# A two-layer cross-attention block on one core: scores of two heads in neighbouring PSUM banks, one exponential for both, and normalised tokens written by GpSimd

## The chip, the core and the metric

The kernel runs on one core of a Trainium2 chip. The metric is device time in microseconds for one launch. Five engines work side by side, each through its own queue in order: TensorE (PE, with its weight loads PEld) multiplies matrices into PSUM, VectorE (DVE) and ScalarE (ACT) read PSUM and SBUF, GpSimd (POOL) works on SBUF, and SyncE (SP) issues DMAs. PSUM has eight banks of 512 float32 columns in each of 128 partitions; each matmul here writes within one bank.

## What is computed

Two layers, each a transformer block with self-attention, cross-attention to a context, and a gated feed-forward part, for 4 batches of 512 tokens of 320 features. There are 20 heads of 16 features. The context has 1601 rows of 192 features.

```python
h1 = _ln(x, n1_g, n1_b)
x = _attn(h1, h1, q1, k1, v1, o1_w, o1_b, heads) + x
h2 = _ln(x, n2_g, n2_b)
x = _attn(h2, context, q2, k2, v2, o2_w, o2_b, heads) + x
h3 = _ln(x, n3_g, n3_b)
a, g = jnp.split(h3 @ ff_w1 + ff_b1, 2, axis=-1)
x = a * jax.nn.gelu(g, approximate=False) @ ff_w2 + ff_b2 + x
```

`_attn` projects q, k and v, takes `softmax(q k^T / 4)` for each head over all keys (512 in self-attention, 1601 in cross-attention), multiplies by v and projects the result. Everything is float32.

## The kernel before

**Units.** The work of a layer is cut into units (L329, L355 to L361): 20 self units and 20 cross units, one for each batch and group of four heads, and then four feed-forward units, one for each batch. `main` (L1196) runs an attention unit, `ff_main` (L1307) a feed-forward unit. An attention unit goes through its keys in chunks of 128: 4 chunks in self-attention, 13 in cross-attention. All 512 queries of the batch are the columns.

**A chunk** has two rounds (L1264), the first for heads 0 and 1, the second for heads 2 and 3. The four heads of a group sit in four slots of 32 partitions, so that matmuls of four heads can run in TensorE at once. A float32 value is split into a high and a low part that lie in neighbouring rows, and a product takes two passes. For a head, `score` (L1202) takes a PSUM bank, writes keys x queries into it in two passes (L1209), subtracts each query's maximum in a third (L1212), and ACT takes the exponential from that bank into a place in SBUF (L1222, 128x512). In the same round two heads of a later unit get a block of the scores from which their maxima are found: two passes on TensorE (L1021) into a bank each, and a reduction on DVE out of it (L1040, 128x512 to 128x1). So the maxima of a unit are ready before the unit begins. The passes of the round's four heads are interleaved by hand (`round_of`, L1186). After the two rounds of a chunk, `values` (L1229) multiplies the exponentials of the chunk *before* with v for all four heads into one bank (L1236); a column of ones beside v gives the sums. ACT copies that bank to a place (L1252, for the first chunk straight into `o`, L1247), and GpSimd adds the place to the unit's `o` (L1253). In the unit ahead of a feed-forward stage (`last`) there are no maxima, all four heads' scores are in one round, and DVE does the adding (L1249).

**What runs beside.** Layer norm, the projections of q, k and v, the transposed context, the division by the sums and the output projection wait in chains of small steps, each with a cost and a due time. `steps` (L460) runs at the end of each chunk and takes steps by due time as long as a credit lasts; a *light* step is a small piece of DVE work, and `steps` is told how many light ones it may take in the chunk (L1276). The order on all engines is therefore written by the program itself; nothing reorders it later.

**Layer norm** (`add_norm`, L521) takes statistics on DVE (L530), a root by Newton steps that run mostly on GpSimd (L503), writes normalised tokens `hn` on DVE (L546, four instructions of 128x320 a batch and stage, with four of 128x64 more ahead of a feed-forward unit), transposes them on TensorE (L559), and ACT puts scale and offset on them out of PSUM (L566). New parts of q and k are copied out by ACT (L818, L848, L892), split into high and low on GpSimd (L699, L700) and moved by DMAs to their slots.

**Banks.** `bank` (L159) takes the bank of the eight that `Pace` (L54) believes free first. `Pace` keeps a running estimate of the time at which each engine reaches each instruction. The choice changes only which bank is taken, not the order of the instructions.

**Places in SBUF.** One ring of places (L230 to L241) serves the exponentials and ACT's copies: 7 of its own with 2 borrowed ones in self-attention, or 5 borrowed ones in cross-attention, where the weights of self-attention are no longer needed. `o` has three buffers.

Of the kernel before, what the change touches and what calls it, by code (L numbers as in the profile page):

```python
# [9 lines left out]
F32 = mybir.dt.float32  # L10
# [43 lines left out]
class Pace:  # L54


    def __init__(self):
# [3 lines left out]
        self.bank_of = {}  # L61
# [4 lines left out]
    def first(self):  # L66
        i = min(range(8), key=lambda i: self.free[i])
        assert self.free[i] < 1e8, self.bank_of
        return i

    def give(self, i, t):
        self.bank_of = {n: k for n, k in self.bank_of.items() if k != i}
        self.bank_of[t.tensor.name] = i
        self.opens[i] = self.free[i]
        self.free[i] = 1e9

    def unread(self, t):
        b = self.bank_of[t.tensor.name]
        self.free[b] = self.ready[b]

    def see(self, r):
        i = r.ins
        kind = type(i).__name__
        banks = {self.bank_of.get(x.bass_ap.tensor.name) for x in list(i.ins) + list(i.outs) if hasattr(x, "bass_ap")}
        banks.discard(None)
# [41 lines left out]
def kernel(ctx: ExitStack, tc: tile.TileContext, x, context, ws, out):  # L127
# [67 lines left out]
    def load_x(b):  # L195
# [40 lines left out]
    at_place = {"kind": "self", "i": -1}  # L236

    def place():
        these = places[at_place["kind"]]
        at_place["i"] = (at_place["i"] + 1) % len(these)  # L240
        return these[at_place["i"]]  # L241
# [160 lines left out]
    def step_bank(shape, name):  # L402
        return bank(name, shape)

    def warm(n):

        ps = step_bank([P, 512], "wps")
        for _ in range(n):
            see(nc.tensor.matmul(ps[:, : 4 * P], lhsT=ident, rhs=fill, start=True, stop=True))
        pace_of.unread(ps)  # L410
# [110 lines left out]
    def add_norm(l, b, i, put, done, due):  # L521
# [19 lines left out]
        def normalise(t):  # L541
# [3 lines left out]
            for to, at, n in ((0, 0, D), (D, D - REST, REST))[: 1 + i // 2]:  # L545
                see(nc.vector.tensor_scalar(  # L546
                    s["hn"][:, t, to : to + n], xb[:, t, at : at + n],
                    s["mv"][:, t, 0:1], s["rstd"][:, t : t + 1], ALU.subtract, ALU.mult,
                ))
            s["round"] = clock["round"]  # L550

        def turn(k, at, n):
# [3 lines left out]
            ps = step_bank([P, N], "hps")  # L556
# [67 lines left out]
    def add_context(l, b, put, due, free):  # L624
# [39 lines left out]
        def tail():  # L664
            ps = step_bank([P, 2, P], "cps")
# [87 lines left out]
    def add_proj(u):  # L753
# [47 lines left out]
        def queries(part):  # L801
            w = N // 2 // parts
            at = [i * (N // 2) + part * w for i in range(2)]
            ps = step_bank([P, 512], "qps")
# [29 lines left out]
        def keys():  # L834

            ps = step_bank([P, 512], "kps")
# [38 lines left out]
        def keys_of_context(i):  # L875

            pss = [bank("kps") for _ in range(4)]
# [705 lines left out]
```

## Time and profile before

| | |
|---|---|
| median of 3 runs | 3033.34 us (3026.81 to 3038.23) |
| the profiled execution's own time | 3038.45 us |
| its span, first to last instruction | 3036.6 us |
| mean granted TensorE clock | 0.989 |
| busy: PE, DVE, ACT, POOL | 2945.4, 2049.5, 1957.7, 1326.4 us |

The stages, by the lines and tiles that are in use: self-attention of the first layer until about 411 us, cross-attention until about 1240, feed-forward until about 1540, then the second layer with self-attention until about 1900, cross-attention until about 2740 and feed-forward to the end.

How to read the rows quoted below: a row of a grouped view has the line, the engine, the operation, what it writes and reads, the shape and the count; then busy us, the mean ns of one, the idle time of the engine just before, and what ended it. A row of the timeline has the start in us, the length, and the instructions merged into it. In TensorE's rows a float32 matmul of the values product counts as two, and a matmul's end is modelled, so that one which is held up looks longer.

### The profile page before, as it was taken

The page shows a single profiled execution, that of the slowest core. Times are in us where ns is not written, and L with a number is a line of the kernel's source. Part 1 is how long each engine was busy: PE and PEld are TensorE (multiplying, and loading weights), DVE is VectorE, ACT ScalarE, POOL GpSimd, SP SyncE. Part 2 cuts the span into 40 slices and gives each one's busy share as a digit, 9 for nine tenths or more (in the row PEclk, how much of TensorE's full clock was granted, in tenths as well). Part 3 has the DMA queues.
Part 4 walks back from the last instruction along what each step waited for, and adds up shares of the span by engine and source line. Part 5 has one row for each costly group of instructions (what it writes and reads, how often), then busy time and mean ns, then how long its engine had stood idle before and what let it go on. Part 6 is the DMA issues. An engine that isn't in the chain of part 4 may idle for free.

```text
span 3036.6 us, 93325 instructions
## 1 busy us (share of the span) xinstructions
PE 2945.4 (97%) x37842; PEld 1609.5 (53%) x37842; DVE 2049.5 (67%) x4011; ACT 1957.7 (64%) x4029; POOL 1326.4 (44%) x1499
## 2 busy tenths in 40 slices
PE   8989999999999999999998999999999999999999
PEld 4445555555555555455554555555555555544555
DVE  6677788888878888422256778778778878873221
ACT  3666667888887888611136775778878878884101
POOL 3456444554555454301124563545645654542100
PEclk8999999999999999999999999999999999999999
DMA  4434222221222221300113332212211221212000
GB/s 101 106 78 95 62 57 47 66 46 45 60 51 57 44 52 25 93 11 0 32 44 76 85 81 59 53 48 42 52 47 35 52 59 33 49 22 73 14 11 13
DMA packets 223751, 157.80 MB, mean 52 GB/s; under 512 B 152724, under 2 KB 187928, under 8 KB 223320
## 3 DMA queue, kind: packets, MB, share of 16 engines
q1 hardware_dynamic: 222440, 150.78, 21.2%
q8 instruction: 297, 4.87, 0.7%
q10 hardware_dynamic: 880, 1.06, 0.2%
q14 instruction: 134, 1.10, 0.1%
HBM read 44.18 MB, written 9.24 MB: 18 GB/s over the span
## 4 chain that ended last, share of the span: by engine, by line
PE 60%; DVE 8%; issue 1%; ACT 1%; SPq 1%; DMA 1%; POOL 0%; ACTq 0%; POOLq 0%; DVEq 0%
PE av L1236 14%; PE fps L1331 9%; PE st L1209 8%; PE sps L1021 7%; PE yps L1386 6%; DVE pm L1040 5%; PE kps L883 3%; PE fps L1344 2%; PE ops L1153 2%; PE st L1212 2%; PE vps L975 2%; PE qps L807 2%; DVE nmax L1040 2%; PE vps L957 1%; PE kps L840 1%
## 5 line engine op out<-in xcount | busy, mean ns | idle before, releaser
L1040 DVE TENSOR_REDUCE pm<-sps 128x1 f32<-128x512 f32 x1920 | 1191.4, 681 | 108.5 <-PE sps L1021 101.4
L1021 PE MATMUL sps<-kT,q 32*128 32x512 f32 (+1 forms) x6400 | 1063.1, 403 | 24.0 <-DMA kT<-stage 6.3
L1222 ACT ACTIVATE pr<-st 128x512 f32<-128x512 f32 (+1 forms) x1710 | 906.4, 603 | 215.1 <-PE st L1212 210.4
L1209 PE MATMUL st<-q,kT 32*128 32x512 f32 (+1 forms) x5440 | 933.0, 435 | 5.3 <-ACT stage L848 2.6
L1253 POOL TENSOR_TENSOR o<-o,pr 128x512 f32<-128x512 f32 x359 | 461.0, 1284 | 656.3 <-ACT pr L1252 638.6
L1209 PEld LDWEIGHTS st<-q,kT 32*128 32x128 f32 (+1 forms) x5440 | 479.0, 180 | 358.1 <-ACT pr L1222 141.7
L1236 PE MATMUL av<-pr,vals 128*32 128x512 f32 (+1 forms) x3420 | 641.5, 614 | 26.4 <-DVE pm L1040 8.8
L1021 PEld LDWEIGHTS sps<-kT,q 32*128 32x128 f32 x6400 | 548.5, 184 | 129.5 <-DVE pm L1040 24.7
L1212 PE MATMUL st<-m,units 32*128 32x512 f32 (+1 forms) x2720 | 533.1, 392 | 11.9 <-DMA m<-turned 11.9
L1222 ACT ACTIVATE wself<-st 128x512 f32<-128x512 f32 (+1 forms) x867 | 463.3, 604 | 80.0 <-PE st L1212 76.3
L1040 DVE TENSOR_REDUCE nmax<-sps 128x1 f32<-128x512 f32 x640 | 397.3, 681 | 163.0 <-PE sps L1021 152.9
L1236 PE MATMUL av<-wself,vals 128*32 128x512 f32 (+1 forms) x1734 | 369.7, 605 | 11.3 <-DVE pm L1040 5.4
L1253 POOL TENSOR_TENSOR o<-o,wself 128x512 f32<-128x512 f32 x191 | 245.2, 1284 | 301.0 <-ACT wself L1252 289.4
L1331 PE MATMUL fps<-hT,w 128*128 128x512 f32 x640 | 283.3, 596 | 0.0
L1354 ACT ACTIVATE pr<-fps,b 128x512 f32<-128x512 f32 x80 | 54.8, 688 | 341.7 <-PE fps L1344 239.4
L1212 PEld LDWEIGHTS st<-m,units 32*128 32x128 f32 (+1 forms) x2720 | 250.8, 181 | 32.5 <-issue 12.0
L1252 ACT COPY pr<-av 128x512 f32<-128x512 f32 x359 | 218.7, 609 | 24.3 <-PE av L1236 24.0
L1331 PEld LDWEIGHTS fps<-hT,w 128*128 128x128 f32 x640 | 118.9, 190 | 148.3 <-issue 147.5
L1236 PEld LDWEIGHTS av<-pr,vals 128*32 128x32 f32 (+1 forms) x3420 | 91.5, 108 | 195.1 <-DVE pm L1040 108.8
L699 POOL TENSOR_SCALAR stage<-stage 128x256 fp32r<-128x256 f32 (+1 forms) x155 | 106.7, 688 | 147.0 <-ACT stage L818 63.2
L883 PEld LDWEIGHTS kps<-ctxT,w 32*128 32x128 f32 (+1 forms) x4992 | 115.7, 163 | 54.5 <-ACT pr L1222 30.2
L1153 PEld LDWEIGHTS ops<-wo,aT 112*32 112x32 f32 (+1 forms) x3072 | 99.0, 110 | 64.2 <-issue 40.2
(99 smaller groups left out, 3076.9 us busy)
## 6 DMA issues: line engine op xcount, KB each, us to landing
q<-stage SPq DMA_DIRECT2D x314, 128.0 KB
kT<-w SPq DMA_DIRECT2D x240, 104.0 KB
aT<-o SPq DMA_DIRECT2D x320, 32.0 KB
kT<-stage SPq DMA_DIRECT2D x156, 64.0 KB
oturn<-over SPq DMA_DIRECT2D x32, 224.0 KB
kT<-w SPq DMA_DIRECT2D x80, 72.0 KB
w<-in_L_xattn_ff_w_dram SPq DMA_DIRECT2D x20, 256.0 KB
m<-turned SPq DMA_DIRECT2D x318, 4.0 KB
```

The costliest lines, as they stand in the source:

```text
L883: see(nc.tensor.matmul(ps[to : to + n, :PIECE], lhsT=wk_q[rows, k, u.g * GD : u.g * GD + n], rhs=first.kvT[rows, k, at : at + PIECE], star ...
L1021: see(nc.tensor.matmul(out, lhsT=u.q[rows, t // 2, e, t % 2 * P : (t % 2 + 1) * P].bitcast(F32R), rhs=u.kT[rows, keys].bitcast(F32R), star ...
L1040: see(nc.vector.tensor_reduce(to[:, j : j + 1], ps, AX.X, ALU.max, negate=(ns == 1)))
L1153: see(nc.tensor.matmul(ps[f : f + m, : D // 2], lhsT=aT[:n, k, t * P + f : t * P + f + m], rhs=wo[:n, k, cols], start=(k == 0), stop=(k == 2),
L1209: see(nc.tensor.matmul(st[:r, :], lhsT=keys, rhs=u.q[rows, :, e].bitcast(F32R), start=(e == 0), stop=False))
L1212: see(nc.tensor.matmul(st[:r, :], lhsT=units_of[rows, :r].bitcast(F32R), rhs=u.mrow[rows, :].bitcast(F32R), start=False, stop=True,))
L1222: see(nc.scalar.activation(p[:r], st[:r], AF.Exp))
L1236: see(nc.tensor.matmul(ps[j * SLOT : (j + 1) * SLOT, :], lhsT=columns_of[:r, head : head + SLOT], rhs=pr.pop((c, j))[:r, :], start=True, s ...
L1252: see(nc.scalar.copy(vo, ps))
L1253: nc.gpsimd.tensor_tensor(u.o, u.o, vo, ALU.add)
L1331: see(nc.tensor.matmul(ps, lhsT=w1[:, k, i * FF + c * P : i * FF + (c + 1) * P], rhs=u.hT[:, k, :], start=ahead and k == 0, stop=not ahead ...
L1386: see(nc.tensor.matmul(ps[:, :D], lhsT=hid[c][:, t * P : (t + 1) * P], rhs=w2[:, c, :], start=(c == 0), stop=(c == NHC - 1),))
```

## The change

Four things are changed together.

1. All of PSUM is one tile of eight banks. `two_banks` takes a pair of neighbouring banks (0-1, 2-3, 4-5 or 6-7): of the four pairs that one whose later bank `Pace` believes free first. `score` handles two heads at once: their scores lie in a pair of banks, the passes keep their order, and one exponential of 128x1024 reads both banks and writes a pair of places. Single banks are taken as before. The feed-forward unit takes its four banks as two pairs.
2. Places are pairs for the exponentials (4 pairs of its own, one more borrowed in cross-attention) and single ones for ACT's copies (2 borrowed in self-attention, 3 in cross-attention), in two rings of their own. The kernel's own places grow from 7 to 8; `o` has two buffers instead of three.
3. `hn` is written by GpSimd, except at the start of the program.
4. `steps` may take two light steps in each chunk; before it was one in a chunk with extra maxima and in a unit's last chunk.

```diff
-    def bank(name, shape=(P, 512)):
+    wide = ps.tile([P, 8, 512], F32, name="ps")
+    pace_of.name = wide.tensor.name
+
+    def taken():
         i = pace_of.first()
-        t = ps.tile(list(shape), F32, tag=f"bank{i}", name=name)
-        pace_of.give(i, t)
-        return t
+        pace_of.give(i)
+        return i
+
+    def bank():
+        return wide[:, taken()]
+
+    def two_banks():
+        i = min(range(0, 8, 2), key=lambda i: max(pace_of.free[i : i + 2]))
+        assert max(pace_of.free[i : i + 2]) < 1e8, pace_of.free
+        for k in (i, i + 1):
+            pace_of.give(k)
+        return [wide[:, i], wide[:, i + 1]], wide[:, i : i + 2]
...
-    own = const.tile([P, 7, N], F32, name="pr")
-    mine = [own[:, i, :] for i in range(7)]
+    own = const.tile([P, 8, N], F32, name="pr")
+    mine = [own[:, i, :] for i in range(8)]
+    spare = wself[:, : 5 * N].rearrange("p (i n) -> p i n", n=N)
+    ours = [own[:, i : i + 2, :] for i in range(0, 8, 2)]
     places = {
-        "self": mine + [w1_flat[:, (2 * KB + 2) * D : (2 * KB + 2) * D + N], w1r[:, 4 * CTX : 4 * CTX + N]],
-        "cross": mine + [wself[:, i * N : (i + 1) * N] for i in range(5)],
+        ("self", "pairs"): ours,
+        ("self", "single"): [w1_flat[:, (2 * KB + 2) * D : (2 * KB + 2) * D + N], w1r[:, 4 * CTX : 4 * CTX + N]],
+        ("cross", "pairs"): ours + [spare[:, 0:2, :]],
+        ("cross", "single"): [spare[:, i, :] for i in range(2, 5)],
     }
...
-                see(nc.vector.tensor_scalar(
+                eng = nc.vector if start["on"] else nc.gpsimd
+                eng.tensor_scalar(
                     s["hn"][:, t, to : to + n], xb[:, t, at : at + n],
                     s["mv"][:, t, 0:1], s["rstd"][:, t : t + 1], ALU.subtract, ALU.mult,
-                ))
+                )
...
-        def score(c, j):
+        def score(c, heads):
             r = min(P, u.nkeys - c * P)
-            rows = slice(j * SLOT, (j + 1) * SLOT)
-            st = bank("st")
+            sts, both = two_banks()
+            rows = [slice(j * SLOT, (j + 1) * SLOT) for j in heads]
...
             def exponential():
-                p = place()
-                see(nc.scalar.activation(p[:r], st[:r], AF.Exp))
-                pr[c, j] = p
+                p = place("pairs")
+                see(nc.scalar.activation(p[:r], both[:r], AF.Exp))
+                for i, j in enumerate(heads):
+                    pr[c, j] = p[:, i, :]
...
-                u.o = three.tile([P, N], F32, tag="o", name="o")
+                u.o = two.tile([P, N], F32, tag="o", name="o")
...
-                vo = place()
+                vo = place("single")
...
-            steps(None, 1 if extra or c == u.nch - 1 else 2)
+            steps(None, 2)
...
-            return [[bank("fps"), bank("fps")] for e in range(2)]
+            return [two_banks()[0] for e in range(2)]
```

More of the change, by code (lines that the diff above doesn't have):

```diff
@@ L400 @@
     start = {"on": True}
-    def step_bank(shape, name):
-        return bank(name, shape)
     def warm(n):
-        ps = step_bank([P, 512], "wps")
+        i = taken()
         for _ in range(n):
-            see(nc.tensor.matmul(ps[:, : 4 * P], lhsT=ident, rhs=fill, start=True, stop=True))
-        pace_of.unread(ps)
+            see(nc.tensor.matmul(wide[:, i, : 4 * P], lhsT=ident, rhs=fill, start=True, stop=True))
+        pace_of.unread(i)
     def yes():
@@ L875, in keys_of_context @@
         def keys_of_context(i):
-            pss = [bank("kps") for _ in range(4)]
+            pss = [bank() for _ in range(4)]
             for k in range(KB):
@@ L970, in values_of_context @@
             w = (h1 - h0) * DH
-            pss = [bank("vps") for _ in range(4)]
+            pss = [bank() for _ in range(4)]
             for k in range(KB):
@@ L1031, in full_two @@
         def full_two(heads, t, s):
-            pss = [bank("sps") for _ in heads]
+            pss = [bank() for _ in heads]
             if ns == 1:
@@ L1047, in rest_two @@
             w = rest + rest % 2
-            pss = [bank("sps") for _ in heads]
+            pss = [bank() for _ in heads]
             todo = [
@@ L1259, in main @@
             if last:
-                round_of([lambda j=j: score(c, j) for j in range(HG)], [])
+                round_of([lambda heads=heads: score(c, heads) for heads in ((0, 1), (2, 3))], [])
                 tick()
@@ L1268, in main @@
                     extra += rounds
-                    round_of([lambda j=j: score(c, j) for j in ((2, 3) if odd else (0, 1))], pair)
+                    round_of([lambda: score(c, (2, 3) if odd else (0, 1))], pair)
             u.scored = c + 1
```

73 lines of the change are left out of this document (40 added, 33 removed).

## The prediction

> **What bounds the kernel now.** I read the page first (busy shares, chain of waits), then the busy times by stage, then one stretch of the cross stage in order of time.
>
> ```profile
> span 3036.6 us, 93325 instructions
> PE 2945.4 (97%) x37842; PEld 1609.5 (53%) x37842; DVE 2049.5 (67%) x4011; ACT 1957.7 (64%) x4029; POOL 1326.4 (44%) x1499
> PE 60%; DVE 8%; issue 1%; ACT 1%; SPq 1%; DMA 1%; POOL 0%; ACTq 0%; POOLq 0%; DVEq 0%
> ```
> ```profile
> 0.00:411.00 411.00, 377.89 (x5400) 202.59 (x5404) 296.10 (x602) 248.24 (x516) 193.15 (x241) 0.94 0.36 84
> 411.00:1240.00 829.00, 810.84 (x12346) 455.80 (x12346) 671.76 (x1310) 678.18 (x1419) 441.70 (x446) 1.00 0.22 50
> 1560.00:1900.00 340.00, 320.64 (x4792) 172.13 (x4788) 250.84 (x485) 230.02 (x476) 170.84 (x204) 0.97 0.33 75
> 1900.00:2740.00 840.00, 823.08 (x12542) 462.50 (x12535) 668.75 (x1280) 684.02 (x1428) 448.05 (x451) 1.00 0.20 46
> ```
>
> The columns of the second fence are PE, PEld, DVE, ACT, POOL. TensorE holds the chain and is busy 97%. The change leaves its matmuls as they are, in number and size, so all it can win is time in which TensorE waits. In the four attention stages (self, cross, self, cross) TensorE is idle for 33.1 + 18.2 + 19.4 + 16.9 = 88 us. Matmuls that are held up look longer, so some waiting hides inside "busy"; the next rows show how much. DVE and ACT are each busy 81 to 82% of the cross stages, so they are close behind.
>
> ```profile
> 673.55 4.99 DVE L1040 TENSOR_REDUCE pm<-sps 128x1 f32<-128x512 f32 x8 [0.29 <-PE sps L1021]
> 673.83 2.07 ACT L1222 ACTIVATE pr<-st 128x512 f32<-128x512 f32 x4 [0.64 <-PE st L1212]
> 674.30 0.62 PE L1236 MATMUL av<-wself,vals 128*32 128x512 f32 x2
> ...
> 675.30 0.44 PE L1209 MATMUL st<-q,kT 32*65 32x512 f32 x2
> ...
> 675.75 0.62 ACT L1252 COPY wself<-av 128x512 f32<-128x512 f32 x1
> ...
> 676.43 0.49 PE L1021 MATMUL sps<-kT,q 32*128 32x512 f32 x1
> 676.45 1.28 POOL L1253 TENSOR_TENSOR o<-o,wself 128x512 f32<-128x512 f32 x1 [1.06 <-ACT wself L1252]
> ...
> 677.08 1.06 PE L1236 MATMUL av<-pr,vals 128*32 128x512 f32 x8
> ...
> 679.60 1.07 PE L1236 MATMUL av<-wself,vals 65*32 65x512 f32 x8
> ...
> 682.39 1.06 PE L1236 MATMUL av<-pr,vals 128*32 128x512 f32 x8
> ```
> ```profile
> 676.42 0.18 PEld L1021 LDWEIGHTS sps<-kT,q 32*128 32x128 f32 x1 [0.15 <-ACT wself L1252]
> ```
>
> These are three plain chunks (four score heads, four maxima, one values product, nothing else). From one values product to the next they take 677.08 - 674.30 = 2.78, then 2.52, then 2.79 us. The 2.78 has a visible cause: one maximum's matmul at 676.43 needs the bank that the values product used, and ACT's copy out of it ends at 675.75 + 0.62 = 676.37. That copy stood behind four exponentials that began at 673.83. DVE's eight reductions take 4.99, 0.62 each, so four are 2.48 us of a 2.52 us chunk: DVE has no room there either.
>
> **The change part by part.**
>
> *One exponential for 1024 columns.* There are 40 self units of 4 chunks and 40 cross units of 13, 680 chunks with two pairs each: 1360 wide exponentials for 2720. No row shows 1024 columns; rows of other widths bound them.
>
> ```profile
> L1222 ACT ACTIVATE pr<-st 128x512 f32<-128x512 f32 x1616 | 857.0, 604 | 209.9 <-PE st L1212 206.7 <-PE sps L1021 0.8 <-ACT pr L1252 0.3
> L818 ACT ACTIVATE stage<-qps 128x128 f32<-128x128 f32 x80 | 24.2, 302 | 4.4 <-PE qps L807 4.2
> L818 ACT ACTIVATE stage<-qps 128x256 f32<-128x256 f32 x40 | 15.4, 384 | 43.9 <-PE qps L807 36.8 <-DMA q<-stage 2.1 <-DVE stage L700 2.0
> ```
>
> From 128 to 256 columns a column costs (384 - 302)/128 = 0.64 ns, from 256 to 512 (604 - 384)/256 = 0.86 ns. So 512 more columns cost 0.33 to 0.44 us. Today the second exponential of a pair costs (2.07 - 0.60)/3 = 0.49 us. A pair saves 0.05 to 0.16 us; I take 0.06, by the nearer row, that of 256 to 512. That frees 1360 x 0.06 = 82 us of ACT, which is not on the path by itself. What counts is the copy, which comes two pairs, 0.12 us, sooner. How often TensorE waits for this copy:
>
> ```profile
>   ACT pr L1252: 8.0, 50
>   ACT wself L1252: 6.0, 38
> ```
>
> These are two rows of the waits of L1021 (us, times): 88 waits. 88 x 0.12 = **-10.6 us**. Bounds: 0, where DVE is late next, and 88 x 0.27 (2.79 less 2.52) = -24. The 26 chunks just before the feed-forward stages have four exponentials in a row and no maxima: 0 to -3, I take -1.5.
>
> [...]
>
> *Banks in pairs.* The exponential gives both banks back together: the first one 0.33 to 0.44 us later than now, the second a little sooner. The next chunk's scores (675.30) start 1.47 us after the first exponential (673.83). The wide one takes 0.60 + 0.44 = 1.04 at most, so 0.43 us is left and nothing waits. In plain chunks banks fall into two halves: two pairs for scores, and four banks for five takers (four maxima, one values product). The second maximum of a chunk then needs the third reduction, due at 673.55 + 3 x 0.62 = 675.41 while the scores start at 675.30: 0.1 us late for one row group, whose next pass has room. Between 0 and 680 x 0.1 = +68; nearest to the rows above, where such lateness is absorbed: **+3**.
>
> *GpSimd writes the normalised tokens.* 128 instructions, of which the four at the start stay on DVE.
>
> ```profile
> L546 DVE TENSOR_SCALAR hn<-x,mv,root 128x320 f32<-128x320 f32 x96 | 53.9, 582 | 21.0 <-POOL root L510 21.0
> L699 POOL TENSOR_SCALAR w<-w 128x416 fp32r<-128x416 f32 x80 | 100.1, 1251 | 19.6 <-DVE w L892 10.1 <-DVE nm L1086 6.0 <-DMA aT<-o 2.4
> L699 POOL TENSOR_SCALAR stage<-stage 128x256 fp32r<-128x256 f32 x75 | 64.1, 855 | 146.0 <-ACT stage L818 62.2 <-ACT stage L848 59.6 <-DMA m<-turned 21.4
> ```
> ```profile
> 963.05 1.29 POOL L1253 TENSOR_TENSOR o<-o,pr 128x512 f32<-128x512 f32 x1 [2.62 <-ACT pr L1252]
> ...
> 963.33 1.55 DVE L546 TENSOR_SCALAR hn<-x,mv,root 128x320 f32<-128x320 f32 x2
> ...
> 964.80 2.47 DVE L1040 TENSOR_REDUCE pm<-sps 128x1 f32<-128x512 f32 x4
> ```
>
> Two of them took 1.55 us beginning inside a GpSimd add that ran until 963.05 + 1.29 = 964.34, and the reductions behind them began only at 964.80. [...] In attention stages 60 of the wide ones leave DVE: 60 x 0.582 = 35 us, and the 21 us that DVE stood waiting for GpSimd's root go as well: 56 us of DVE time. The feed-forward ones gain nothing, since TensorE has no wait there. What of the 56 was TensorE's time? All of it in a plain chunk (DVE full), little in a chunk with a projection. I take a little over a third, **-20**; bounds 0 and -56.
>
> GpSimd gains 92 of 320 columns and 32 of 64. One column costs (1251 - 855)/160 = 2.48 ns: 1.01 us and 0.38 us, together 105 us, or twice that if the second operation doubles it (44% busy becomes 47 to 51%). Behind them in its queue stand the adds into o, and the parts of q and k whose transfers feed later maxima. With three places (cross) or two (self) for the copies, ACT's copy waits for the add two chunks back at the earliest: 5.3 us after a copy (2.78 + 2.52), where the add ends 677.73 - 675.75 = 2.0 us after it. Two normalisations (2.0) and one split (some 1.6) just fill the 3.3 us between. The transposes of 24 token blocks may wait up to 1.2 us (two instructions, 1.01 less 0.44 each): 0 to +28, **+4**.
>
> [...]
>
> *The rest, at nothing.* The feed-forward stages take the same four banks a time, as two pairs. Two light steps in each chunk only shift small VectorE work by a chunk. Two buffers for o instead of three: a self unit takes 411/20 = 20.5 us, so a whole unit lies between o's transfers and its next use; without that cover 80 copies on ACT would wait.
>
> Sum: -10.6 - 1.5 + 3 - 20 + 4 = **-25 us**. The profiled execution took 3038.45 us (span 3036.6): 3013. The median of the runs, 3033.34, is 5.1 lower, so I forecast **3008 us**.
>
> **Rivals.**
> *More than forecast*: ACT's and DVE's lateness feed each other (a late reduction delays the values product, and that its copy). All plain chunks then run at 2.52: -24, with -45 from DVE: 3033 - 69 = 2964. For it: the 2.52 exists. Against it: DVE's 2.48 stays.
> *Nothing*: DVE's reductions still end last in plain chunks and normalisation falls mostly into chunks with room: 0 to -10, about 3028.
> *Slower, pairs come late*: once ACT is over 0.43 us behind, a score pair waits for the whole wide exponential, and maxima, copies and projections that broke up a pair delay it further. Price 0.1 to 0.2 us in 200 to 400 chunks: +20 to +80, about 3073. For it: ACT at 82% in the cross stages. Against it: 0.43 us of room in the row above.
> *Slower, GpSimd late*: its queue delays q, k and the copies; 24 blocks x 1 to 2 us = +24 to +48, about 3060. Against it: GpSimd idle over half the span.
>
> **How the numbers follow.** About 0.5% (15 us) is what a measurement of this kernel can tell from no change. Forecast (2990 to 3018): 0.42. More: 0.16. Nothing (3018 to 3048): 0.23. Pairs late: 0.13. GpSimd late: 0.06. Faster 0.58, same 0.23, slower 0.19. The range 2965 to 3055 takes in "more" down to its price and most of the GpSimd case, and leaves out the dearer half of the pair case. The forecast's own range is 2990 to 3018.
>
> **What would show it.** Right: wide exponentials of 0.93 to 1.04 us; plain chunks at 2.55 to 2.7; no wait of L1021's successor for the copy over 0.1 us; DVE over 54 us less busy (92 x 0.582), GpSimd about 105 more. Wrong: score matmuls waiting for exponentials; transposes waiting for GpSimd; copies on ACT waiting for adds; an exponential over 1.09 us (0.60 + 0.49), which would make ACT slower.

## The result, and the profile after

The changed kernel takes 3048.34 us (median of 6 runs, 3045.38 to 3052.62), the kernel before 3034.48 us (6 runs on the same chip, 3026.81 to 3038.23). The ratio is 1.0049, 95% interval 1.0035 to 1.0063: **slower by about 15 us**. Forecast were 3008 us and 25 us less than before, so 40 us separate forecast and result. The time is inside the range that was given (2965 to 3055).

The page of the changed kernel begins so (its own time is 3048.70 us; line numbers are those of the changed file: 16 higher for the normalised tokens, L562, the transposes, L575, the maxima, L1037 with reductions in L1056, and the scores, L1225; 23 for the subtraction of the maximum, L1235, and the exponential, L1245; 24 for the values product, L1260, its copy, L1276, and the add into o, L1277):

```profile
span 3046.9 us, 91851 instructions
...
PE 2918.6 (96%) x37842; PEld 1620.0 (53%) x37842; DVE 1995.4 (65%) x3887; ACT 1883.5 (62%) x2669; POOL 1470.2 (48%) x1623
...
PE 79%; DVE 12%; POOL 3%; issue 2%; ACT 1%; SPq 1%; DMA 1%; ACTq 0%; DVEq 0%; POOLq 0%
```

ACT is busy 1957.7 - 1883.5 = 74 us less (82 forecast), VectorE 54 us less (54 forecast), GpSimd 144 us more (105 forecast). So the engines that stood close behind TensorE were relieved as planned, and TensorE is still idle 3046.9 - 2918.6 = 128 us where it was idle 3036.6 - 2945.4 = 91. Not all of these 37 us are lost time: its busy time fell by 27 us with the same 37842 matmuls, so some waiting that looked busy before is in sight now. In the chain of waits GpSimd is new, with 3%. VectorE's 12% is not a growth over the 8% of before, since that chain's shares add up to only 72%, of which 8 are 11%.

The same three plain chunks as shown of before, in order of time:

```profile
679.06 1.07 PE L1260 MATMUL ps<-pr,vals 128*32 128x512 f32 x8
...
680.28 0.58 ACT L1276 COPY wself<-ps 128x512 f32<-128x512 f32 x1
...
680.83 5.01 DVE L1056 TENSOR_REDUCE pm<-ps 128x1 f32<-128x512 f32 x8 [0.19 <-PE ps L1037]
...
681.12 1.94 ACT L1245 ACTIVATE pr<-ps 128x1024 f32<-128x1024 f32 x2 [0.26 <-PE ps L1235]
...
681.58 0.62 PE L1260 MATMUL ps<-pr,vals 65*32 65x512 f32 x2
...
684.25 1.06 PE L1260 MATMUL ps<-pr,vals 128*32 128x512 f32 x8
...
686.77 1.07 PE L1260 MATMUL ps<-pr,vals 128*32 128x512 f32 x8
```

From one values product to the next they take 2.52, 2.67 and 2.52 us, against 2.78, 2.52 and 2.79. Four heads' exponentials take 1.94 us where they took 2.07. Eight reductions still take 5.01 us: VectorE's 2.5 us a chunk stay. Summed over all 215 plain chunks of the two traces, start to start of the values products, they take 582 us after and 600 before: the plain chunks did gain, 17 us. But the 16 chunks that hold transposes and nothing else beside scores, values and maxima take 90 us where they took 65, which gives 25 back, and the chunks with a projection of queries, keys or values and no transposes take 1163 us (271 of them) where they took 1154 (272).

The waits of TensorE (us in total, times, longest) before, two rows, and after:

```profile
PE av L1236 <- DVE pm L1040: 14.1, 24, 1.1
...
PE hps L559 <- DVE hn L546: 1.8, 1, 1.8
```
```profile
PE ps L1260 <- DVE pm L1056: 34.6, 104, 1.8
PE ps L575 <- POOL hn L562: 20.2, 15, 2.4
...
PE ps L1235 <- DMA m<-turned: 10.0, 7, 4.4
PE ps L1037 <- DMA q<-stage: 6.5, 3, 5.8
PE ps L1037 <- DMA kT<-stage: 5.4, 3, 4.0
```

Two waits are new in size. The values product waits for a maximum's reduction 104 times instead of 24, 34.6 us instead of 14.1. And the transposes wait for GpSimd's normalised tokens 15 times, 20.2 us, where they waited 1.8 us for VectorE's.

One block's normalised tokens, in order of time:

```profile
2041.91 2.87 POOL L562 TENSOR_SCALAR hn<-x,mv,root 128x320 f32<-128x320 f32 x2
...
2044.72 0.44 PE L575 MATMUL ps<-ident,hn 128*112 128x128 f32 x2
2044.74 1.27 POOL L1277 TENSOR_TENSOR o<-o,wself 128x512 f32<-128x512 f32 x1
...
2045.99 2.85 POOL L562 TENSOR_SCALAR hn<-x,mv,root 128x320 f32<-128x320 f32 x2
...
2047.48 0.32 PE L575 MATMUL ps<-ident,hn 128*112 128x128 f32 x1 [2.32 <-POOL hn L562]
...
2048.89 1.40 PE L575 MATMUL ps<-ident,hn 128*112 128x128 f32 x8 [1.09 <-POOL hn L562]
```

Two token blocks go to GpSimd in one chunk (2.87 us), an add into o stands behind them (1.27 us), then come the next two (2.85 us): 7 us of work, begun at 2041.91 and ended at 2048.84. TensorE reaches the transposes at 2044.72, does the two blocks that are ready, and waits 2.32 us for the third and 1.09 us for the fourth.

The clock that TensorE is granted drops as well. The first row is the stretch around these transposes in the changed kernel, the second the same place in e4, a run below in which no tokens are written there. The last three figures of a row are the granted clock, the DMA share and GB/s:

```profile
2043.00:2056.00 13.00, 9.58 (x132) 5.96 (x130) 6.53 (x14) 7.53 (x11) 11.50 (x11) 0.87 0.01 3
```
```profile
2020.00:2040.00 20.00, 19.83 (x355) 12.95 (x351) 13.36 (x30) 15.65 (x24) 12.63 (x19) 1.00 0.08 29
```

In the changed kernel's trace the granted clock is 0.50 from 2049.5 on for 3.4 us:

```profile
2049.50:2052.90 3.40, 3.40 (x26) 2.32 (x24) 1.19 (x2) 2.57 (x4) 3.40 (x5) 0.50 0.02 2
```

The trace has such a stretch at 0.50, of 3.4 or 6.8 us, at each of the six groups of transposes that waited 2.4 us or more for GpSimd in all, and none at the two that waited 1.3 and 0.4 us (1.00 there); e4 has none at any of them. The changed kernel's trace has 13 more elsewhere, and that of the kernel before 15 in all, so longer waits at the transposes are not all that goes with one.

What one instruction takes, by form:

```profile
L1245 ACT ACTIVATE pr<-ps 128x1024 f32<-128x1024 f32 x1088 | 1066.9, 1022 | 313.5 <-PE ps L1235 306.4 <-PE ps L1037 1.0 <-ACT pr L1245 0.3
...
L562 POOL TENSOR_SCALAR hn<-x,mv,root 128x320 f32<-128x320 f32 x92 | 131.8, 1437 | 1.1
...
L562 POOL TENSOR_SCALAR hn<-x,mv,root 128x64 f32<-128x64 f32 x32 | 18.5, 579 | 0.0
```

The wide exponential takes 1.02 us, inside the 0.93 to 1.04 that was named. GpSimd's normalised tokens take 1.44 us, not 1.01: a column costs (1437 - 579)/256 = 3.35 ns, where the one-operation instruction from which it was estimated costs 2.48.

### The profile page after: what moved, and what is told of

Read it like the earlier page. It is cut to its first block, busy times and chain, and to the rows that moved or that the text cites. A ratio compares the mean times of both kernels' runs of the same rounds, so it can differ in the third digit from the quotient of the medians.

```text
span 3046.9 us, 91851 instructions
## 1 busy us (share of the span) xinstructions
PE 2918.6 (96%) x37842; PEld 1620.0 (53%) x37842; DVE 1995.4 (65%) x3887; ACT 1883.5 (62%) x2669; POOL 1470.2 (48%) x1623
## 3 DMA queue, kind: packets, MB, share of 16 engines
q10 hardware_dynamic: 880, 1.06, 0.2%
## 4 chain that ended last, share of the span: by engine, by line
PE 79%; DVE 12%; POOL 3%; issue 2%; ACT 1%; SPq 1%; DMA 1%; ACTq 0%; DVEq 0%; POOLq 0%
PE ps L1260 20%; PE ps L1225 12%; PE ps L1037 10%; PE ps L1355 9%; DVE pm L1056 6%; PE ps L1410 6%; PE ps L899 4%; PE ps L1169 3%; PE ps L823 3%; DVE nmax L1056 3%; PE ps L991 3%; PE ps L1235 3%; PE ps L1368 2%; PE ps L973 2%; POOL hn L562 1%
## 5 line engine op out<-in xcount | busy, mean ns | idle before, releaser
L1245 ACT ACTIVATE pr<-ps 128x1024 f32<-128x1024 f32 (+1 forms) x1152 | 1129.9, 1021 | 321.0 <-PE ps L1235 309.9
L1056 DVE TENSOR_REDUCE pm<-ps 128x1 f32<-128x512 f32 x1920 | 1192.6, 682 | 112.2 <-PE ps L1037 101.5
L1037 PE MATMUL ps<-kT,q 32*128 32x512 f32 (+1 forms) x6400 | 1040.9, 402 | 18.1 <-DMA q<-stage 6.5
L1225 PE MATMUL ps<-q,kT 32*128 32x512 f32 (+1 forms) x5440 | 923.9, 436 | 8.1 <-ACT pr L1245 2.4
L1277 POOL TENSOR_TENSOR o<-o,wself 128x512 f32<-128x512 f32 x458 | 587.9, 1284 | 682.2 <-ACT wself L1276 654.9
L1260 PE MATMUL ps<-pr,vals 128*32 128x512 f32 (+1 forms) x4608 | 734.0, 614 | 53.8 <-DVE pm L1056 27.1
L1225 PEld LDWEIGHTS ps<-q,kT 32*128 32x128 f32 (+1 forms) x5440 | 479.3, 181 | 358.7 <-ACT pr L1245 188.1
L1037 PEld LDWEIGHTS ps<-kT,q 32*128 32x128 f32 x6400 | 558.4, 186 | 91.9 <-issue 18.4
L1235 PE MATMUL ps<-m,units 32*128 32x512 f32 (+1 forms) x2720 | 545.8, 394 | 10.4 <-DMA m<-turned 10.0
L1056 DVE TENSOR_REDUCE nmax<-ps 128x1 f32<-128x512 f32 x640 | 397.5, 683 | 174.0 <-PE ps L1037 158.6
L1276 ACT COPY wself<-ps 128x512 f32<-128x512 f32 x458 | 270.4, 590 | 24.2 <-DVE pm L1056 13.9
L1235 PEld LDWEIGHTS ps<-m,units 32*128 32x128 f32 (+1 forms) x2720 | 261.3, 182 | 30.5 <-issue 11.4
L1260 PEld LDWEIGHTS ps<-pr,vals 128*32 128x32 f32 (+1 forms) x4608 | 105.3, 108 | 278.5 <-DVE pm L1056 163.5
L1245 ACT ACTIVATE wself<-ps 128x1024 f32<-128x1024 f32 (+1 forms) x208 | 212.4, 1021 | 49.5 <-PE ps L1235 45.9
L1260 PE MATMUL ps<-wself,vals 128*32 128x512 f32 (+1 forms) x832 | 219.6, 606 | 10.0 <-DVE pm L1056 7.5
L562 POOL TENSOR_SCALAR hn<-x,mv,root 128x320 f32<-128x320 f32 x124 | 149.2, 1216 | 1.1
L1277 POOL TENSOR_TENSOR o<-o,w1r 128x512 f32<-128x512 f32 x58 | 74.2, 1280 | 137.6 <-ACT w1r L1276 137.4
```

The source lines that it names most:

```text
L562: eng.tensor_scalar(s["hn"][:, t, to : to + n], xb[:, t, at : at + n], s["mv"][:, t, 0:1], s["rstd"][:, t : t + 1], ALU.subtract, ALU.mult,)
L1037: see(nc.tensor.matmul(out, lhsT=u.q[rows, t // 2, e, t % 2 * P : (t % 2 + 1) * P].bitcast(F32R), rhs=u.kT[rows, keys].bitcast(F32R), star ...
L1056: see(nc.vector.tensor_reduce(to[:, j : j + 1], ps, AX.X, ALU.max, negate=(ns == 1)))
L1225: see(nc.tensor.matmul(st[:r, :], lhsT=u.kT[at, u.k0 + u.cols[c] : u.k0 + u.cols[c] + r].bitcast(F32R), rhs=u.q[at, :, e].bitcast(F32R), s ...
L1235: see(nc.tensor.matmul(st[:r, :], lhsT=units_of[at, :r].bitcast(F32R), rhs=u.mrow[at, :].bitcast(F32R), start=False, stop=True,))
L1245: see(nc.scalar.activation(p[:r], both[:r], AF.Exp))
```

## The experiments

Two theories to begin with. **G**: the move of the normalised tokens to GpSimd costs what the change lost, by the transposes' wait. **B**: the banks in pairs or the light steps cost it. All runs are compared with the kernel before on the same chip (medians of 3034 to 3038 us); 0.1% is 3 us.

| run | median, us | ratio to before | 95% interval |
|---|---|---|---|
| the change | 3048.34 | 1.0049 | 1.0035 to 1.0063 |
| e1_hn_vector | 3040.59 | 1.0019 | 1.0009 to 1.0029 |
| e2_before_hn_gpsimd | 3047.91 | 1.0041 | 1.0027 to 1.0055 |
| e3_before_no_hn | 3023.09 | 0.9957 | 0.9943 to 0.9971 |
| e4_after_no_hn | 3021.61 | 0.9954 | 0.9939 to 0.9968 |
| e5_lights_only | 3033.40 | 0.9987 | 0.9978 to 0.9997 |
| e6_pairs_wide_only | 3043.80 | 1.0027 | 1.0015 to 1.0040 |
| e7_pairs_narrow | 3077.09 | 1.0133 | 1.0117 to 1.0149 |
| e8_late_turn | 3047.65 | 1.0038 | 1.0024 to 1.0052 |
| e9_pairs_narrow_same_banks | 3049.80 | 1.0050 | 1.0036 to 1.0064 |
| e10_lights_split_hn | 3027.02 | 0.9970 | 0.9958 to 0.9982 |
| e11_after_split_hn | 3028.57 | 0.9973 | 0.9963 to 0.9982 |
| e12_odd_bank_first | 3028.99 | 0.9979 | 0.9970 to 0.9988 |
| e13_pair_if_free | 3028.76 | 0.9962 | 0.9949 to 0.9976 |
| e14_pair_if_near | 3027.05 | 0.9959 | 0.9947 to 0.9972 |

### The normalised tokens alone

e1 is the changed kernel with the tokens back on VectorE, e2 the kernel before with them on GpSimd:

```
 e1, against the changed kernel
-                eng = nc.vector if start["on"] else nc.gpsimd
-                eng.tensor_scalar(
+                eng = nc.vector
+                see(eng.tensor_scalar(
...
 e2, against the kernel before
-                see(nc.vector.tensor_scalar(
+                eng = nc.vector if start["on"] else nc.gpsimd
+                eng.tensor_scalar(
```

> The changed kernel with the normalised tokens written by VectorE again; wide exponentials, paired banks and two light steps stay. Theory G (the loss is GpSimd's: 1.44 us for one normalisation instead of the 1.01 that I estimated, and TensorE stands ahead of the transposes): the 26 us of gaps between transposes go and VectorE's holding up of reductions comes back, so 3012 to 3025 us, below the kernel before by 0.3 to 0.7%. Theory B (paired banks hold up scores and maxima as often as the wide exponential helps, and the normalisation is about even): 3043 to 3055, no better than the changed kernel.

> The kernel before with only the normalised tokens moved to GpSimd. Theory G: 20 to 35 us slower than the kernel before, 3054 to 3070. Theory B: within 8 us of it, 3026 to 3042.

e2 is 12.5 us slower than before (0.41%), e1 0.30% or 9 us faster than the changed kernel. So G holds for the sign in both kernels, though by less than it said (20 to 35 us for e2). The place shows in e2's waits too, where the number of light steps is the old one:

```profile
PE hps L560 <- POOL hn L547: 16.1, 11, 2.9
```

But e1 isn't faster than before, it is 0.19% or 6 us slower: what remains of the change loses too, and B holds as well. Neither theory was enough.

In e3 and e4 the tokens aren't written again after the start, in the kernel before and in the changed one; all later transposes read the first ones:

```
...
+            if not start["on"]:
+                s["round"] = clock["round"]
+                return
```

> The kernel before, which writes the normalised tokens only for the first batch and layer and lets all later transposes read those; everything else runs. It sizes what the 124 instructions cost on VectorE in all: my prediction says 20 us (3014); if VectorE had room in most of the chunks concerned, under 10 us (3024 or more). Theories G and B don't differ here.

> The changed kernel with the same part left out (normalised tokens only for the first batch and layer). Theory G: the gain of paired banks and wide exponentials stands bare, 3000 to 3015, some 10 to 15 us under the kernel before without these instructions. Theory B: 3035 to 3050, above the kernel before without these instructions.

On VectorE the tokens cost 0.43% or 13 us in the kernel before, and 0.19 + 0.46 = 0.65% or 20 us in the changed one (e1 against e4). So the 20 us which the move was to win were there to be won in the changed kernel. On GpSimd the same tokens cost 0.49 + 0.46 = 0.95% or 29 us (the change against e4). Set beside e4 chunk by chunk, the changed kernel falls back by 3.6 to 5.2 us at each of six groups of transposes and by 1.7 at a seventh, 28 us in all: with the tokens on GpSimd, nearly the whole price is at the transposes. The waits for GpSimd are 20.2 us of it. The mean granted clock is 0.987 in the changed kernel's runs and 0.990 in e4's; as an estimate, 1.3% of 3047 us less 1.0% of 3020 us leaves 9 us for the clock, and the two make 29. That the waits bring the clock down fits all of these rows, but no run holds the clock and leaves the waits.

e3 and e4 are level (0.9957 and 0.9954). Neither theory said that: with no tokens to write, the rest of the change neither gains nor loses.

### Making the transposes later, or the tokens sooner

e8 writes the tokens ahead of the feed-forward stages on VectorE and places the other transposes later in the order:

```
-                eng = nc.vector if start["on"] else nc.gpsimd
+                eng = nc.vector if start["on"] or i == 2 else nc.gpsimd
...
-                may_overwrite if k == 0 else yes, lambda: clock["round"] >= s["round"] + 1,
+                may_overwrite if k == 0 else yes, lambda: clock["round"] >= s["round"] + (1 if start["on"] or i == 2 else 5),
```

> The changed kernel in which the normalised tokens ahead of the feed-forward stages are written on VectorE, and the other transposes are placed at least five rounds instead of one after the last of their normalised tokens on GpSimd. If what the move to GpSimd costs is TensorE waiting at the transposes (theory G, 24 us of such waits), most of it goes: 3021 to 3030, near the 3021.6 of the changed kernel without later normalisations. [...]

That was a miss: it is 0.11% under the changed kernel, inside what the two intervals leave open. Rows of its waits of TensorE:

```profile
PE ps L1235 <- DMA m<-turned: 16.4, 9, 3.5
...
PE ps L1037 <- DMA kT<-stage: 12.1, 6, 4.3
PE ps L1037 <- DMA q<-stage: 6.6, 3, 5.8
...
PE ps L575 <- DVE hn L562: 0.6, 1, 0.6
```

The transposes wait 0.6 us in all, for VectorE, and none of the rows names GpSimd. But the projections of q and k hang on the transposes, and their transfers now come late: the three DMA rows hold 16.4 + 12.1 + 6.6 = 35.1 us, against 10.0 + 5.4 + 6.5 = 21.9 in the changed kernel. Waits for exponentials, copies and reductions grew by some 12 us more, so together they take back the 20 us saved: the wait was moved, not removed. That the later transposes are the cause of all of these is argued from the order of the work; e8 also moves the tokens ahead of the feed-forward stages, so it isn't a test of the lateness alone.

e10 and e11 leave the order as it is and give GpSimd only the first two of the four token blocks, in the kernel before (with two light steps a chunk) and in the changed one:

```
-                eng = nc.vector if start["on"] else nc.gpsimd
-                eng.tensor_scalar(
+                here = start["on"] or t >= 2
+                done_by = (nc.vector if here else nc.gpsimd).tensor_scalar(
...
```

> The kernel before with two light steps in every chunk, and with the normalised tokens of the first two of four token blocks on GpSimd, of the last two on VectorE. In the changed kernel the chunks without transposes became about 17 us shorter when the normalised tokens moved to GpSimd, and the transposes waited 26 us longer. If these are two separate effects, half the move keeps about half the first and none of the second: 5 to 10 us under before, 3025 to 3031. If the time that GpSimd takes is a price by itself: at or above the run with the light steps alone, 3033 or more.

> The changed kernel with the same split: two token blocks on GpSimd, two on VectorE. If the two effects are separate: 5 to 10 us under the changed kernel with all of them on VectorE, so 3030 to 3036, and no wait of a transpose for GpSimd over 0.3 us. If GpSimd's time is the price: between that and the changed kernel, 3041 to 3049.

Both came out on the side of two separate effects, e11 with more than was expected of it: it is 0.46% or 14 us under e1, where 5 to 10 were named, 0.76% or 23 us under the changed kernel, and faster than before. Rows of its waits of TensorE (this file's lines are 2 higher):

```profile
PE ps L1262 <- DVE pm L1058: 33.9, 102, 1.7
...
PE ps L577 <- DVE hn L562: 0.4, 1, 0.4
PE ps L577 <- POOL hn L562: 0.2, 1, 0.2
```

The transposes' wait for GpSimd is 0.2 us instead of 20.2. The first row is as in the changed kernel, and so belongs to something else. e10 and e11 are level (0.9970 and 0.9973): they differ only in the pairs, the width, the places and the buffers for o, which together neither gain nor lose here.

### The light steps

e5 is the kernel before with two light steps in every chunk, `steps(None, 2)`, and nothing else. e6 is e1 with the old number of light steps, so pairs of banks and places, the wide exponential and two buffers for o.

> The kernel before with one edit of the change alone: two light steps in every chunk, also in the last chunk of a unit and where a unit carries extra work (before: one there). Normalised tokens stay on VectorE, narrow exponentials stay. The changed kernel with its normalised tokens back on VectorE took 5.3 us more than before (3040.6 against 3035.3), so something else of the change costs what the wide exponential gains. Theory L: the light steps bunch small VectorE work ahead of reductions; this run is then 3 to 8 us slower than before, 3038 to 3043. Theory P: the banks in pairs cost it; this run is then within 3 us of before, 3032 to 3038.

> The changed kernel with its normalised tokens on VectorE and with one light step where before had one: what is left of the change is banks and places in pairs, the wide exponential, and two buffers for o. Theory L (light steps cost what the wide exponential gains): 3025 to 3035, so at or below before. Theory P (banks in pairs cost it): as with the light steps, 3038 to 3043.

e5 is 0.13% or 4 us faster than before, and e6 is 0.27% or 8 us slower. Theory L falls: the light steps gain a little. What loses in e1 is what e6 keeps, so theory P, or the places and buffers that come with the pairs.

### The pairs and the width apart

e7 and e9 are e6 with two exponentials of 512 columns for each pair of banks. e7 lets the kernel's own bank times, which choose the next bank, follow the narrow exponentials; e9 writes the wide one's times into them, so that the banks change hands in exactly the order of e6:

```
-                see(nc.scalar.activation(p[:r], both[:r], AF.Exp))
...
+                    see(nc.scalar.activation(p[:r, i], sts[i][:r], AF.Exp))
 e9, in place of that line
...
+                    one_exp = nc.scalar.activation(p[:r, i], sts[i][:r], AF.Exp)
...
+                pace_of.pair(one_exp)
```

> As the run with pairs and the wide exponential alone, but with two exponentials of 512 columns for each pair of banks in place of one of 1024: isolates the width from the pairing. If the width is worth what plain chunks show (13 to 17 us shorter in sum in the changed kernel), this run is 8 to 15 us slower than the one with wide exponentials. If the width is worth nothing and the plain chunks gain from the order of banks, the two agree within 3 us.

> As the run with pairs and the wide exponential alone, with two exponentials of 512 columns for each pair of banks, and with the choice of banks exactly as with the wide one (the narrow run before it chose its banks by the narrow exponentials' own due times, so that there banks changed hands differently as well). If the width itself is worth what that run showed: 30 us or more over the wide one, so 3070 or more. If most of the 33 us there was the choice of banks: 10 to 15 us over the wide one (1360 pairs, each 0.06 us less of ACT, 82 us in all, of which a part is on the path), 3053 to 3060.

Both lie outside what was expected. e7 alone would have said that the width is worth 1.06%, 32 us. e9 says 0.50 - 0.27 = 0.23%, 7 us. The other 25 us of e7 are the choice of banks, and by the two traces the plain chunks alone take 27 us more. The rows of the score matmuls' weight loads, by form, of e9 and of e7 (busy, mean ns, idle before them and what ended it):

```profile
L1231 PEld LDWEIGHTS ps<-q,kT 32*128 32x128 f32 x5120 | 475.4, 183 | 355.9 <-ACT pr L1252 169.3 <-issue 59.2 <-ACT wself L1252 43.0
```
```profile
L1225 PEld LDWEIGHTS ps<-q,kT 32*128 32x128 f32 x5120 | 452.9, 184 | 417.4 <-ACT pr L1246 160.7 <-issue 55.1 <-DVE pm L1056 51.2
```

In e7 the score pairs get banks that a maximum held, and wait for its reduction: 51.2 us, a releaser that isn't among the first three in e9. Over all weight loads and matmuls of the line it is 68 us in e7, 30 in e9, 29 in e6 and 18 in the kernel before. That is like the rival "pairs come late", with maxima in the place of exponentials. Weight loads run beside matmuls (in the changed kernel they are busy 1620.0 us beside 2918.6 of matmuls, in a span of 3046.9), so these need not be us of the kernel's time.

Against before, e9 is the price of pairs of banks and places and of two buffers for o, with nothing from the width: 0.50% or **15 us**. Its waits of TensorE, and the row of before that answers to the second:

```profile
PE ps L1267 <- DVE pm L1062: 23.3, 48, 1.1
...
PE ps L1231 <- DVE pm L1062: 5.6, 9, 1.0
```
```profile
PE st L1209 <- DVE pm L1040: 1.0, 1, 1.0
```

The values product waits 23.3 us for a maximum's bank (14.1 before), the scores 5.6 (1.0 before): 13.8 us more, about the 15. The chunks lengthen everywhere a little: those with a projection by 4 us, the plain ones by 2, all others together by 7. With the wide exponential (e6) the values product's row is:

```profile
PE ps L1260 <- DVE pm L1056: 33.8, 102, 1.2
```

The wait grows by 10.5 us while the time falls by 7. By chunks this comes apart. The plain chunks take 591 us in e6 and 601 in e9, so the width gains 10 us there, and this wait still grows there from 4.8 to 7.5 us: TensorE gets sooner to the same late reduction and waits in sight. The 272 chunks with a projection take 1171 us in e6 and 1158 in e9, so they lose 13, and there the wait grows from 11.5 to 19.4. A longer wait in the view can be a longer time or not; the length of the chunk tells.

### Lifting the pairs

e12 takes a single bank, among those free by then, from the pair whose other bank stays in use longest. e13 and e14 take a pair for scores only where both its banks are free as soon as any two (e14: within 0.3 us), and else two lone banks with two narrow exponentials. All three stand on e11.

```
 e12
...
+        now = max(self.at["PE"], self.free[i])
+        return max((j for j in range(8) if self.free[j] <= now), key=lambda j: self.free[j ^ 1])
 e13 (e14: + 0.3)
+            second = max(sorted(pace_of.free)[1], pace_of.at["PE"])
+            if max(pace_of.free[i : i + 2]) > second + 0.0:
+                return [bank(), bank()], None
...
```

> The split version of the changed kernel in which a single bank is taken, among those that are free by then, from the pair whose other bank is in use the longest, so that whole pairs stay free for scores. If what the pairs cost is score matmuls waiting for a bank that a maximum or a values product holds: 10 to 25 us under the split version, so 3010 to 3026. If it is maxima that have only four banks left: no gain, or slower by up to 10 us.

> The split version of the changed kernel, in which a score pair takes neighbouring banks only if these are by the kernel's own bank times free as soon as any two banks, and else two lone banks with two exponentials of 512 columns (about a third of the pairs keep the wide exponential). If the binding to pairs costs the 15 us: the pairing's price goes, and a third of the width's gain stays: 10 us or more under the split version, 3010 to 3020. If the price is elsewhere (places, buffers, order): 3028 to 3035, since only some of the width's 7 us is lost.

> The same with 0.3 us of grace, so that about half of the pairs keep the wide exponential. If the binding to pairs is the price: between the run without grace and the split version, or below both where the width's gain weighs more, 3012 to 3024. If the price is elsewhere: 3028 to 3033.

e12 gains nothing (0.9979 against e11's 0.9973): keeping pairs whole for the scores isn't what is missing. e13, with the first of these rows among TensorE's waits and the second by form, is 0.11% under e11, less than the intervals tell apart and less than the 10 us expected:

```profile
PE ps L1269 <- DVE pm L1062: 18.8, 43, 1.7
```
```profile
L1252 ACT ACTIVATE pr<-ps 128x1024 f32<-128x1024 f32 x361 | 363.6, 1027 | 76.3 <-PE ps L1241 74.9
```

By the words of its expectation this is the outcome "the price is elsewhere"; e14 lies between its two. The rows say more. The values product's wait falls from 33.9 us (102 times) to 18.8 (43 times), nearly to before's 14.1. Part of this fall comes with the narrow exponentials alone, since e9, fully bound, waits 23.3. What the binding costs shows better in the chunks, in e10 (no pairs), e11 (pairs, all wide) and e13 (lone banks where these are free sooner; 471 of 1360 pairs wide):

| | e10 | e11 | e13 |
|---|---|---|---|
| 215 plain chunks, us | 598.5 | 587.8 | 592.8 |
| 271 chunks with a projection, no transposes, us | 1152.5 | 1163.9 | 1153.3 |

Pairs with the wide exponential gain 11 us in the plain chunks and lose 11 in those with a projection, which take up to four more single banks. Without the binding the loss is gone. With two thirds of the pairs narrow about half of the gain is gone too, and the other chunks take 3 us more; that leaves the 3 us between e11 and e13. e13 keeps the places and the two buffers for o, so they don't make this loss. These sums are of one trace for each run. But of the runs with 271 or 272 such chunks, all with wide exponentials on bound pairs have 1163 to 1171 us in them, those with narrow ones and e13 have 1147 to 1159, and e14, with 876 pairs wide, has 1161. What remains open is the part of e9's 15 us that is spread over all chunks; the places and buffers may hold some of it. e13 and e14 are the fastest versions tried that leave nothing out: 0.9962 and 0.9959 of before.

## Why the prediction was wrong

The step that failed first of all is the price of GpSimd at the transposes, put at +4 us where the runs show 25 to 29; the second is the banks in pairs, put at +3. The terms of the sum against what the runs gave (differences of ratios, each good to about 5 us):

| step | forecast, us | measured, us | from |
|---|---|---|---|
| wide exponential (-10.6 - 1.5) | -12 | -7 | e6 less e9 |
| banks in pairs (with places, two buffers for o) | +3 | +15 | e9 against before |
| tokens off VectorE | -20 | -20 | e4 less e1 |
| GpSimd late, transposes | +4 | +29 | the change less e4 |
| light steps | 0 | -2 (e5: -4) | e1 less e6 |
| sum | -25 | +15 | the change against before |

The five differences add up to the whole by the way they are formed, so the last row is no check of the others. They also depend on the order. If the tokens are moved first, they cost 13 us on VectorE (before less e3) and 25 on GpSimd (e2 less e3), and the rest of the change adds 2 (the change less e2). The price at the transposes is large either way. The price of the pairs is not: with all tokens on VectorE the pairs and the width lose 10 us (e1 less e5), with none or half of them there they are nearly level (e4 against e3, e11 against e10). Why the net is a loss only then was not tested; it fits that VectorE's reductions, which give the banks back, come later with the tokens in its queue.

- **"The transposes ... may wait ... +4"** is the step that decided. The mechanism, its place and even its bound (0 to +28) were in the text, and the wait was among its signs of being wrong; the value taken was the wrong end, and with +29 in its place the forecast is 0. Three things failed in the working. The duration: the two-operation instruction takes 1.44 us, not the estimated 1.01 from the one-operation row, though the text itself named a dearer second operation and left it out of the transposes' wait. And the queue: I counted two instructions' extra time (1.2 us) as if GpSimd were free between them. In the stretch shown two blocks (2.87 us) and an add (1.27) come into a chunk of about 2.7, so GpSimd falls behind, and the transposes come one round after the last block. And the clock: the sum had no term for it, and about 9 of the 29 us are TensorE at a lower granted clock, by the estimate above.
- **The price of one instruction.** GpSimd takes 1437 ns (L562, after) where VectorE takes 582 in the mean (L546, before) for the same 128x320 instruction, with one tensor input and two pointer scalars. The 0.44 us that the step sets against 1.01 is VectorE's middle time in the kernel before: its 128 instructions of both widths took 302, 439 and 1535 ns (least, middle, longest), the 96 wide ones 440 in the middle.
- **"banks in pairs: +3"** was mis-sized within its bounds (0 to +68), and looked for in the wrong chunks. "Four banks for five takers" was worked out for the plain chunks, which lose only 2 us by the pairs alone (e9) and gain with the width. The loss is mostly where a projection takes single banks as well, and it is the values product that waits there, not the second maximum: it gets the bank of a maximum not yet reduced.
- **"-20 for the tokens"** holds in size, as what the tokens cost on VectorE in the changed kernel; in the kernel before it is 13. That their price there is VectorE's time and not TensorE's transposes is shown by e11, which moves half of them and gains 14 us.
- **Wide exponential**: 1.02 us as forecast, 74 us off ACT. In the plain chunks e6 is 10 us under e9, and in the 26 chunks ahead of the feed-forward stages 2, near the -10.6 and -1.5 of the sum. But the chunks with a projection, of which the working said nothing, took back 13, and the net over the whole kernel is 7 by the medians, between the bounds 0 and -24. Of the 17 us that the plain chunks gained in all, only 9 came with pairs and width (600 us before, 591 in e1); the other 8 came with the tokens off VectorE (591 in e1, 583 in e4 and 582 in the changed kernel).
- The rivals "GpSimd late" (0.06) and "pairs come late" (0.13) were near in subject and off in place: GpSimd's lateness reached TensorE at the transposes, not through the copies or q and k, and the pairs' at the values product, not at the scores. I had also treated them as exclusive, each large enough to decide alone; two losses of 12 and 25 us over what the sum held for them came together.
- Two slips in the working change nothing: 0.49 less 0.44 is 0.05 us a pair, not 0.06 (74 us over 1360 pairs is 0.054), and VectorE is busy 80 to 81% of the cross stages, not 81 to 82%.

## What to carry to other kernels

Work that was moved to a slower engine here (1437 ns an instruction against 582) saved the 20 us that it cost on the old one and cost 29, nearly all of it at its readers: count everything that engine's queue takes in between the first and the last piece, and set it against TensorE's time from there to the reader. Moving part of it, the pieces that are read first (here two of four), kept 14 of the 20 us with a wait of 0.2 us (e11); placing the reader later gained nothing here, with transfers due behind it (e8). Here the constraint on buffers (neighbouring banks) was charged to the last taker of the rest, in the chunks with the most takers, so look there before the gain on the constrained side is counted. Terms measured one at a time need not add: the same pairs and width cost 10 us with the tokens on VectorE and next to nothing with half of them on GpSimd. And the granted clock fell to 0.50 for 3.4 or 6.8 us at the six longer waits for GpSimd here (2.4 to 3.5 us), so such a wait may cost more than its own length.

## What the runs showed of the hardware that was not expected

- The granted clock was 0.50 for 3.4 or 6.8 us at each of the six groups of transposes in the changed kernel that waited 2.4 to 3.5 us in all, and at none of the two that waited 0.4 and 1.3. In e2 (mean granted clock of its runs 0.986) it was so at the four groups that waited 2.9 to 3.3 us, and at none of the four that waited 0.3 to 2.0.
- GpSimd's subtract-and-multiply with two pointer scalars costs 3.35 ns a column (1437 ns at 320, 579 at 64), its one-operation form 2.48 ns (1251 at 416, 855 at 256).
- One exponential over two neighbouring banks takes 1022 ns, 1.69 times the 604 of one bank alone, but only 0.06 us less than two of 512 back to back: 1.94 us for four heads against 2.07.
- The choice of banks is worth more than the width: with the same instructions in pairs of banks with narrow exponentials the kernel took 1.33% more than before with one choice (e7, 3077 us) and 0.50% more with another (e9, 3050 us).
